# Four graph layers in one kernel: the opening's loads and order, the place of one division, and the engine of the last folds

## The chip, the cores and the metric

The kernel runs on one core of one Trainium2 chip. A core has five engines with an instruction queue each: TensorE (PE, its weight loads shown apart as PEld), VectorE (DVE), ScalarE (ACT), GpSimd (POOL) and SyncE (SP), which here only issues transfers. They run side by side and wait for one another through semaphores. The metric is the time on the device in microseconds (us), the median of several runs; lower is better.

## The reference

The input x is (8, 2048, 64): 8 graphs of 2048 nodes with 64 features, and one adjacency matrix `adj` (2048, 2048) of zeros and ones. Each of four layers normalises x over the features, applies a ReLU, computes a graph layer and adds its result to x.

```python
h = jnp.maximum(_layernorm(x, axis=-1), 0.0)
x = x + _L0_gnn_ref(h, H, adj, 64, W, W_ind, a_node, a_gn, a_ge, fcW, fcb, av)
...
h = jnp.maximum(_layernorm(x, axis=-1), 0.0)
x = x + _L3_gnn_ref(h, adj, embedding, weight, bias)
```

What matters of layer 0 and layer 3 here:

```python
# layer 0
industry = jnp.einsum('nm,bmf->bnf', adj / deg, x @ W_ind)
...
coefs1 = jax.nn.softmax(logits2, axis=-1)          # over the hyperedges e of node n
g = jnp.einsum('bne,benf->bnf', coefs1, all_he)
# layer 3
w = jnp.einsum('nd,dkio->nkio', embedding, weight)  # d = 16, k = 3
b = jnp.einsum('nd,do->no', embedding, bias)
As = [eye, A, 2.0 * (A @ A) - eye]
x_g = jnp.einsum('knm,bmc->bnkc', jnp.stack(As, 0), x)
out = jnp.einsum('bnki,nkio->bno', x_g, w) + b
```

Layer 1 is an attention over the neighbours, layer 2 three steps of a message passing with a small MLP.

## The kernel before

Nodes are cut into 16 tiles of 128 (NT = 16) and into 4 chunks of 512 columns (NCW = 4, CW = 512); the 8 graphs go in 4 pairs (NP = 4), since 2 x 64 features fill 128 partitions. The kernel is one long unrolled program. A scheduler places the instructions, except where order is kept by hand: through `InOrder` wrappers (V, A, G, S for VectorE, ScalarE, GpSimd, SyncE) and, for TensorE, through `kit.mm` and `kit.turn` while `kit.strict` is set. Transfers that SyncE and ScalarE issue go to their own queues[...].

**Opening** (lines 957 to 1071, in `layer0`). A loop over j normalises the x tiles (each 128 nodes x 8 graphs x 64 features), multiplies them by W_ind, splits the product into a rounded high part and a low rest, and multiplies both with the first 512 columns of the transposed adjacency matrix. One iteration j works on several tiles, each step with its own lag: `sums` and `centred` of tile j (VectorE, GpSimd), `squares`, `sums2`, `scales`, `scaled` of tile j-1 (ScalarE, VectorE), `turns` and `turned` of tile j-2 (four transposes on TensorE, copies on ScalarE), `maps` of tile j-3 (eight matmuls `py`), `halves` of tile j-4 (the split: a copy on ScalarE, then a subtraction on VectorE), and `spread` of tile j-5: eight matmuls into `acc`, each high part followed by its low rest, and one into `deg0` for the degrees. The tuple of steps is run in this order in every iteration, and each engine keeps to it. The row tiles `at` of the adjacency matrix come through GpSimd's queue, five of them in the pool; a new one is issued every second iteration.

The same loop makes the bias of layer 3, embedding times bias, as four chunks: `biases(c)` is 4 matmuls of a 16-row piece of the transposed embedding `eT[c]` with `bw` (each fp32 matmul is two instructions in the trace, as are the maps), and ScalarE copies the chunk from PSUM to `bs[c]`, right behind `squares`. The four `eT` come by four transfers (two on SyncE, two on ScalarE), into buffers of the list pool. The chunks use the four PSUM banks that `acc` takes over at j = 5.

**Pair lists** (`pairs_of` to `done`, loop from line 1441). 18 tiles of 114 nodes with 3 blocks of pairs each, 54 blocks. For each block: matmuls, `mixed` (two VectorE operations, one exponential on ScalarE), `weighed` (one VectorE operation and a product, on GpSimd for all but the last two blocks, which stay on VectorE), `gathered` (two instructions on TensorE, `pgs`, 5 blocks behind). After a tile's three gathers, `divided` multiplies by a reciprocal on VectorE (`gn`), `back` turns it (`ptg`), `done` copies to `hn`. The gather of a tile needs the PSUM buffer (one of two) that the division of the tile before last sets free. The division of tile 15 (LT - 3) stands at j = last + 2, behind the weighing of block 53.

**Kernel's end** (`layers23`, lines 2224 to 2287). For each graph pair p and node tile i, the weight products `u` are multiplied by the embedding on VectorE, added up to `fold` (lines 2269 to 2280), and three more additions on GpSimd (lines 2281 to 2283) end in `ot`, which SyncE stores. After all that, lines 2344 to 2348 sum up `kit.bad`, which tells whether the inputs are of the kind that the kernel is made for, and write `flag`. Each engine reads the flag (line 2349) and branches over a general version of the kernel, which is not run here. Line 2390 is the program's common end.

Of the kernel before, what the change touches and what calls it, by code (L numbers as in the profile page):

```python
# [8 lines left out]
FP = mybir.dt.float32  # L9
FR = mybir.dt.float32r  # L10
AF = mybir.ActivationFunctionType
# [5 lines left out]
P = 128  # L17
# [14 lines left out]
def cols(c, w=CW):  # L32
    return slice(c * w, (c + 1) * w)
# [742 lines left out]
def layer0(kit, hn, x1_dram, open_early, late_tile, between):  # L776
# [64 lines left out]
    with ExitStack() as sA:  # L841
# [115 lines left out]
        with ExitStack() as s1:  # L957
            sb = s1.enter_context(tc.tile_pool(name="nf_sb", bufs=2, reuse_waits="tile"))
            ps = s1.enter_context(tc.tile_pool(name="nf_ps", bufs=2, space=PSUM, reuse_waits="tile"))
            bw = lst.tile([P, B * F + 2 * B], FP, tag="hlo", name="bw", bufs=3)[0:16, 0:P]  # L960
            eT, pbs, bs = [], accs(), []
            for c in range(NCW):
                if c < 3:
                    eT.append(lst.tile([P, B * F + 2 * B], FP, tag="hhi", name="eT", bufs=3)[0:16, 0:CW])
                    bs.append(sb.tile([P, CW], FP, tag="bs", name="bs", bufs=3))
                else:
                    eT.append(lst.tile([P, B * F + 2 * B], FP, tag="hlo", name="eT", bufs=3)[0:16, 0:CW])
                    bs.append(lst.tile([P, B * F + 2 * B], FP, tag="hlo", name="bs", bufs=3)[:, 0:CW])

            def biases(c):  # L970
                for k in range(4):
                    kit.mm(pbs[c][:, k * P : (k + 1) * P], eT[c][:, k * P : (k + 1) * P], bw, start=True, stop=True)

# [59 lines left out]
            kit.use_ln_exp()  # L1033
            load(0)
            for h in range(2):
                A.dma_start(out=bw[:, half(h)], in_=t["L3_gnn_bias"])
            for c in range(NCW):
                (A if c > 1 else S).dma_start(out=eT[c], in_=t["embT"][:, cols(c)])
            for i in range(1, 4):
                load(i)  # L1040
            for g in range(2):
                at[g] = rows_of(0, g)
            kit.strict = True
            for j in range(NT + 5):
                on = lambda k: 0 <= j - k < NT
                for c in {1: (0, 1), 3: (2,), 4: (3,)}.get(j, ()):
                    biases(c)
                if j == 5:
                    acc = accs()
                if 9 <= j < 9 + NCW:  # L1050
                    S.dma_start(out=kit.bias_dram[:, cols(j - 9)], in_=bs[j - 9])
                if 1 <= j < 4:
                    at[j + 1] = rows_of(0, j + 1)
                if 0 < j and j + 3 < NT:
                    load(j + 3)
                if j == 6:
                    first = loads()
                for lag, step in (
                    (0, sums), (0, centred), (1, squares), (1, sums2), (3, maps), (4, halves),
                    (1, scales), (1, scaled), (2, turns), (2, turned), (5, spread),  # L1060
                ):
                    if on(lag):
                        step(j - lag)
                    if j in (1, 2, 4, 5) and step is squares:
                        c = j - 1 - j // 4
                        A.activation(bs[c], pbs[c], AF.Copy)
                m = j - 5
                if m > 0 and m % 2 and m // 2 + 5 < NT // 2:
                    at[m // 2 + 5] = rows_of(0, m // 2 + 5)
# [243 lines left out]
    with ExitStack() as s0:  # L1313
# [125 lines left out]
        for j in range(last + 2 * NB):  # L1439
# [13 lines left out]
            if 1 <= j <= last:  # L1453
                mixed(j - 1)
            if 3 <= j < last + 3:
                weighed(j - 3)
            if j == last + 2:
                divided(LT - 3)
                back(LT - 4)
# [547 lines left out]
def layers23(self, aT):  # L2007
# [181 lines left out]
    for p in range(NP):  # L2189
# [32 lines left out]


        y1 = sb.tile([P, N], FP, tag="y1", name="y1", bufs=1)
        yn, after = [None] * NCW, [None] * NCW
# [8 lines left out]
        for c in range(2, NCW):  # L2234
            acc = ps.tile([P, CW], FP, tag="acc", name="acc")
            spread(acc, y, c, True, every)
            nc.scalar.copy(y1[:, cols(c)], acc)
            weave.start(again(y1, c, yn))
        xn = None
        for c in range(NCW):  # L2240
# [13 lines left out]
            for k in range(4):  # L2254
# [24 lines left out]
                for h in range(2):  # L2279
                    nc.vector.tensor_add(fold[:, h], pr[h][:, 0:4, :], pr[h][:, 4:8, :])  # L2280
                nc.gpsimd.tensor_add(fold[:, :, 0:2, :], fold[:, :, 0:2, :], fold[:, :, 2:4, :])  # L2281
                nc.gpsimd.tensor_add(ot, fold[:, :, 0, :], fold[:, :, 1, :])  # L2282
                nc.gpsimd.tensor_add(ot, ot, xr[:, ks].rearrange("p (h f) -> p h f", h=2))
                nc.sync.dma_start(
# [11 lines left out]
def four_layers(  # L2296
# [13 lines left out]
    with ExitStack() as s:  # L2310
        keep = s.enter_context(tc.tile_pool(name="keep_f", bufs=1))
        dram = s.enter_context(tc.tile_pool(name="x_dram", bufs=1, space=DRAM))
        x1, x3 = (dram.tile([NP, P, N], FP, name=f"xd{k}") for k in (1, 3))
        kit = Kit(tc, t, keep)
        kit.bias_dram = dram.tile([P, N], FP, name="bias_dram")
        low = s.enter_context(tc.tile_pool(name="hn_f", bufs=1, reuse_waits="tile"))
# [26 lines left out]
        later[0].run(aT)  # L2343
        ps = s.enter_context(tc.tile_pool(name="flag_ps", bufs=1, space=PSUM))
        nc.vector.tensor_reduce(kit.bad[:, 0:1], kit.bad, AX.X, OP.add)
        pb = ps.tile([F, 1], FP, name="pbad")
        nc.tensor.matmul(pb, kit.ones, kit.bad[:, 0:1], start=True, stop=True)
        nc.vector.tensor_scalar(flag, pb[0:1, :], 0.5, None, op0=OP.is_lt)
    with tc.If(nc.values_load(flag[0:1, 0:1]) < 1):
# [44 lines left out]
```

## Time and profile before

| what | us |
|---|---|
| median of 3 runs | 1881.71 (1881.08 to 1883.15) |
| the profiled execution | 1880.27 |
| its span | 1878.1 |
| TensorE busy | 1840.7 |
| VectorE busy | 1174.5 |
| first spread of the opening begins | 23.55 |
| last division of the pair lists begins | 356.09 |
| last operation of VectorE ends | 1868.05 |

Busy time says how long an engine had an instruction in work. In a line of the order of time stand the start, the time, the engine, the source line (632 is that of the ordering wrapper, 737 that of `kit.mm`, 744 that of `kit.turn`), the operation, the tile written and the tiles read, the shape and the count, and in brackets how long the engine had been idle before it and what ended that. A line of the waits has who waited, for whom, us in total, times and the longest. "DMA" stands for a transfer. "POOLq" or "SPq" is the instruction sequencer of that engine: reads of the flag, branches, semaphores, the issue of transfers.

### The profile page before, as it was taken

The page shows a single profiled execution, that of the slowest core. Times are in us where ns is not written, and L with a number is a line of the kernel's source. Part 1 is how long each engine was busy: PE and PEld are TensorE (multiplying, and loading weights), DVE is VectorE, ACT ScalarE, POOL GpSimd, SP SyncE. Part 2 cuts the span into 40 slices and gives each one's busy share as a digit, 9 for nine tenths or more (in the row PEclk, how much of TensorE's full clock was granted, in tenths as well). Part 3 has the DMA queues.
Part 4 walks back from the last instruction along what each step waited for, and adds up shares of the span by engine and source line. Part 5 has one row for each costly group of instructions (what it writes and reads, how often), then busy time and mean ns, then how long its engine had stood idle before and what let it go on. Part 6 is the DMA issues. An engine that isn't in the chain of part 4 may idle for free.

```text
span 1878.1 us, 26150 instructions
## 1 busy us (share of the span) xinstructions
PE 1840.7 (98%) x10364; PEld 1146.9 (61%) x10364; DVE 1174.5 (63%) x1843; ACT 463.1 (25%) x1048; POOL 311.7 (17%) x435
## 2 busy tenths in 40 slices
PE   8999999899999999999999999999999999999997
PEld 7877767443333333577765577855677755777653
DVE  7766699789999999932446732357523275524465
ACT  5422455572222221121301112200112101113000
POOL 4211387220000000000111200012100021101122
PEclk9999999999999999999999999999999999999999
DMA  7666395383222222142101022101122011121000
GB/s 205 186 185 207 103 284 144 107 208 79 54 61 52 63 57 57 46 99 67 51 13 28 22 69 62 34 23 26 43 62 62 12 30 28 54 65 51 5 20 12
DMA packets 86372, 142.60 MB, mean 76 GB/s; under 512 B 33800, under 2 KB 34056, under 8 KB 83568
## 3 DMA queue, kind: packets, MB, share of 16 engines
q1 hardware_dynamic: 64976, 80.64, 14.8%
q0 software_dynamic: 21040, 56.98, 12.4%
q10 hardware_dynamic: 224, 3.22, 0.5%
q8 instruction: 83, 1.36, 0.3%
q14 instruction: 49, 0.40, 0.1%
HBM read 106.85 MB, written 37.09 MB: 77 GB/s over the span
## 4 chain that ended last, share of the span: by engine, by line
PE 50%; issue 10%; DMA 2%; POOL 2%; DVE 1%; POOLq 0%; ACT 0%; SPq 0%; DVEq 0%
PE acc L737 31%; PE u L737 14%; PE py L737 2%; PE pv L737 1%; POOL fold L2281 1%; PE var L737 1%; PE mean L737 1%; DMA xd<-e 0%; DMA W3f<-in_L_gnn_weight 0%; DMA den<-d_dram 0%; PE tx L744 0%; POOL ot L2282 0%; PE tv L744 0%; PE tp L744 0%; DVE pt L1807 0%
## 5 line engine op out<-in xcount | busy, mean ns | idle before, releaser
L737 PE MATMUL acc<-aT,parts 128*128 128x512 f32 x1664 | 441.3, 409 | 0.0
L737 PEld LDWEIGHTS acc<-aT,parts 128*128 128x128 f32 x1664 | 306.6, 188 | 97.7 <-issue 39.2
L737 PE MATMUL o<-pt,hS 128*32 128x512 f32 x2048 | 247.1, 593 | 2.0 <-DVE pt L632 1.2
L737 PE MATMUL u<-W3f,y 64*128 64x512 f32 x1024 | 241.3, 589 | 0.0
L2269 DVE TENSOR_TENSOR pr<-u,embf 128x512 f32<-128x512 f32 x256 | 170.6, 687 | 109.8 <-PE u L737 103.1
L1807 DVE SCALAR_TENSOR_TENSOR pt<-R,wd,aT 128x1024 f32<-128x1024 f32 x188 | 230.0, 1276 | 8.5 <-DMA R<-r_dram 5.2
L737 PEld LDWEIGHTS u<-W3f,y 64*128 64x128 f32 x1024 | 100.0, 187 | 119.8 <-issue 119.8
L737 PEld LDWEIGHTS o<-pt,hS 128*32 128x32 f32 x2048 | 79.1, 110 | 143.8 <-issue 112.8
L737 PE MATMUL dn<-pt,vd 128*32 128x512 f32 x1024 | 134.9, 593 | 0.0
L737 PE MATMUL u<-W3f,v 64*128 64x512 f32 x512 | 133.0, 596 | 0.0
L2281 POOL TENSOR_TENSOR fold<-fold 128x256 f32<-128x256 f32 x64 | 47.8, 746 | 495.8 <-DVE fold L2280 495.8
L2060 DVE TENSOR_TENSOR yb<-py,cb_f 128x512 f32<-128x512 f32 x32 | 22.1, 691 | 157.9 <-PE py L737 157.9
L1106 PE MATMUL acc<-at,Y 128*128 128x512 f32 x384 | 101.7, 405 | 0.3 <-ACT ev L1136 0.2
L737 PE MATMUL acc<-aTl,parts 128*128 128x512 f32 x384 | 99.7, 398 | 0.0
L2157 POOL TENSOR_TENSOR bq<-bq,xp 128x512 f32<-128x512 f32 x16 | 20.7, 1293 | 421.9 <-ACT xp L2140 421.9
L2273 DVE TENSOR_TENSOR pr<-pr 128x512 f32<-128x512 f32 x128 | 88.0, 688 | 2.2
L737 PEld LDWEIGHTS u<-W3f,v 64*128 64x128 f32 x512 | 56.5, 186 | 49.6 <-issue 36.3
L1807 DVE SCALAR_TENSOR_TENSOR pt<-R,wd,aTl 128x1024 f32<-128x1024 f32 x64 | 79.3, 1280 | 8.6 <-PE dn L737 3.9
L737 PEld LDWEIGHTS dn<-pt,vd 128*32 128x32 f32 x1024 | 40.7, 110 | 67.7 <-issue 49.2
L737 PEld LDWEIGHTS acc<-aTl,parts 128*128 128x128 f32 x384 | 71.5, 188 | 16.2
L1106 PEld LDWEIGHTS acc<-at,Y 128*128 128x128 f32 x384 | 68.5, 188 | 14.1 <-issue 0.8
L2074 DVE TENSOR_TENSOR parts<-tp,parts 128x512 fp32r<-128x512 f32 x16 | 11.1, 692 | 85.3 <-ACT parts L2073 85.3
(374 smaller groups left out, 2683.0 us busy)
## 6 DMA issues: line engine op xcount, KB each, us to landing
at<-in_adjT POOLq DMA_DIRECT2D x32, 512.0 KB, 4.6
raw<-in_adjT SPq DMA_DIRECT2D x64, 256.0 KB, 3.3
aT<-in_adjT POOLq DMA_DIRECT2D x12, 1024.0 KB, 7.5
xp<-xd SPq DMA_DIRECT2D x45, 256.0 KB, 2.9
R<-r_dram SPq DMA_DIRECT2D x14, 512.0 KB, 3.8
hhi<-hi_dram POOLq DMA_DIRECT2D x18, 235.1 KB, 4.3
hlo<-lo_dram POOLq DMA_DIRECT2D x18, 235.1 KB, 4.4
hi_dram<-hi SPq DMA_DIRECT2D x16, 264.0 KB, 3.1
```

The lines of the kernel that those rows point to most:

```text
L737: one = self.nc.tensor.matmul(*args, **kw)
L1106: mm(acc[p], Y[h][:, m, p, :], at[:, k, :], start=m + h == 0, stop=m == NT - 1 and h == 1)
L1807: V.scalar_tensor_tensor(pt, R, w, a.bitcast(FP), op0=OP.max, op1=OP.mult)
L2060: nc.vector.tensor_tensor(yb, py, bias[:, None, :].to_broadcast([P, 4, P]), op=OP.add)
L2074: nc.vector.tensor_tensor(lo, tp, hi.bitcast(FP), op=OP.subtract)
L2157: nc.gpsimd.tensor_add(bq, bq, xp)
L2269: nc.vector.tensor_tensor(a, u[h], emb[:, i, 8 * w : 8 * w + 8, None].to_broadcast([P, 8, F]), op=OP.mult)
L2273: nc.vector.tensor_add(pr[h], pr[h], a)
L2281: nc.gpsimd.tensor_add(fold[:, :, 0:2, :], fold[:, :, 0:2, :], fold[:, :, 2:4, :])
```

## The change

The opening: the embedding comes in one transfer of 16 rows into the memory of `M` (which is loaded only after the loop), at the head of ScalarE's queue; the four first x tiles lead SyncE's; the spread lags four tiles, not five, so that the loop has one iteration less; in iteration 1 the steps of the old tile come before `sums` and `centred` of the new one; the bias chunks are made in iterations 1 to 3 and copied in iterations 1 to 4. The pair lists' end: the division of tile 15 goes from j = last + 2, behind the weighing of block 53, to j = last, between `mixed` of block 53 and the weighing of block 51. The kernel's end: the last three additions are on VectorE for the last node tile of the last graph pair alone; the sum of `kit.bad` and the flag are made ahead of the last graph pair's last stage, in a PSUM buffer of that stage.

```diff
@@ -958,18 +958,16 @@
             sb = s1.enter_context(tc.tile_pool(name="nf_sb", bufs=2, reuse_waits="tile"))
             ps = s1.enter_context(tc.tile_pool(name="nf_ps", bufs=2, space=PSUM, reuse_waits="tile"))
             bw = lst.tile([P, B * F + 2 * B], FP, tag="hlo", name="bw", bufs=3)[0:16, 0:P]
-            eT, pbs, bs = [], accs(), []
+            eT, pbs, bs = M.rearrange("p t h e -> p (t h e)")[0:16], accs(), []
             for c in range(NCW):
                 if c < 3:
-                    eT.append(lst.tile([P, B * F + 2 * B], FP, tag="hhi", name="eT", bufs=3)[0:16, 0:CW])
                     bs.append(sb.tile([P, CW], FP, tag="bs", name="bs", bufs=3))
                 else:
-                    eT.append(lst.tile([P, B * F + 2 * B], FP, tag="hlo", name="eT", bufs=3)[0:16, 0:CW])
                     bs.append(lst.tile([P, B * F + 2 * B], FP, tag="hlo", name="bs", bufs=3)[:, 0:CW])
 
             def biases(c):
-                for k in range(4):
-                    kit.mm(pbs[c][:, k * P : (k + 1) * P], eT[c][:, k * P : (k + 1) * P], bw, start=True, stop=True)
+                for k in range(4 * c, 4 * c + 4):
+                    kit.mm(pbs[c][:, (k % 4) * P : (k % 4 + 1) * P], eT[:, k * P : (k + 1) * P], bw, start=True, stop=True)
 
             deg0 = ps.tile([P, CW], FP, tag="deg0", name="deg0", bufs=1)
             groups = lambda a: a.rearrange("p (g f) -> p g f", f=F)
@@ -1031,22 +1029,18 @@
                 kit.mm(deg0, ones_r, at[m // 2][:, m % 2, :], start=m == 0, stop=m == NT - 1)
 
             kit.use_ln_exp()
-            load(0)
+            A.dma_start(out=eT, in_=t["embT"])
             for h in range(2):
                 A.dma_start(out=bw[:, half(h)], in_=t["L3_gnn_bias"])
-            for c in range(NCW):
-                (A if c > 1 else S).dma_start(out=eT[c], in_=t["embT"][:, cols(c)])
-            for i in range(1, 4):
+            for i in range(4):
                 load(i)
             for g in range(2):
                 at[g] = rows_of(0, g)
             kit.strict = True
-            for j in range(NT + 5):
+            for j in range(NT + 4):
                 on = lambda k: 0 <= j - k < NT
-                for c in {1: (0, 1), 3: (2,), 4: (3,)}.get(j, ()):
+                for c in {1: (0, 1), 2: (2,), 3: (3,)}.get(j, ()):
                     biases(c)
-                if j == 5:
-                    acc = accs()
                 if 9 <= j < 9 + NCW:
                     S.dma_start(out=kit.bias_dram[:, cols(j - 9)], in_=bs[j - 9])
                 if 1 <= j < 4:
@@ -1055,16 +1049,18 @@
                     load(j + 3)
                 if j == 6:
                     first = loads()
-                for lag, step in (
-                    (0, sums), (0, centred), (1, squares), (1, sums2), (3, maps), (4, halves),
-                    (1, scales), (1, scaled), (2, turns), (2, turned), (5, spread),
-                ):
+                inputs, rest = [(0, sums), (0, centred)], [
+                    (1, squares), (1, sums2), (3, maps), (4, halves),
+                    (1, scales), (1, scaled), (2, turns), (2, turned), (4, spread),
+                ]
+                for lag, step in rest + inputs if j == 1 else inputs + rest:
+                    if j == 4 and step is spread:
+                        acc = accs()
                     if on(lag):
                         step(j - lag)
-                    if j in (1, 2, 4, 5) and step is squares:
-                        c = j - 1 - j // 4
-                        A.activation(bs[c], pbs[c], AF.Copy)
-                m = j - 5
+                    if 0 < j < 5 and step is squares:
+                        A.activation(bs[j - 1], pbs[j - 1], AF.Copy)
+                m = j - 4
                 if m > 0 and m % 2 and m // 2 + 5 < NT // 2:
                     at[m // 2 + 5] = rows_of(0, m // 2 + 5)
             kit.strict = False
@@ -1452,10 +1448,11 @@
                 next_nodes(i + 2)
             if 1 <= j <= last:
                 mixed(j - 1)
+            if j == last:
+                divided(LT - 3)
             if 3 <= j < last + 3:
                 weighed(j - 3)
             if j == last + 2:
-                divided(LT - 3)
                 back(LT - 4)
             if 5 <= j < last + 5:
                 gathered(j - 5)
@@ -2221,6 +2218,8 @@
             y = yn
 
 
+        if p + 1 == NP:
+            nc.vector.tensor_reduce(kit.bad[:, 0:1], kit.bad, AX.X, OP.add)
         y1 = sb.tile([P, N], FP, tag="y1", name="y1", bufs=1)
         yn, after = [None] * NCW, [None] * NCW
 
@@ -2236,6 +2235,10 @@
             spread(acc, y, c, True, every)
             nc.scalar.copy(y1[:, cols(c)], acc)
             weave.start(again(y1, c, yn))
+        if p + 1 == NP:
+            pb = ps.tile([P, CW], FP, tag="u0", name="pbad")
+            mm(pb[0:F, 0:1], kit.ones, kit.bad[:, 0:1], start=True, stop=True)
+            nc.vector.tensor_scalar(kit.flag, pb[0:1, 0:1], 0.5, None, op0=OP.is_lt)
         xn = None
         for c in range(NCW):
             xr = chunk_of(x3_dram[p], c)
@@ -2278,9 +2281,10 @@
                 ot = sb.tile([P, 2, F], FP, tag="ot", name="ot", bufs=1)
                 for h in range(2):
                     nc.vector.tensor_add(fold[:, h], pr[h][:, 0:4, :], pr[h][:, 4:8, :])
-                nc.gpsimd.tensor_add(fold[:, :, 0:2, :], fold[:, :, 0:2, :], fold[:, :, 2:4, :])
-                nc.gpsimd.tensor_add(ot, fold[:, :, 0, :], fold[:, :, 1, :])
-                nc.gpsimd.tensor_add(ot, ot, xr[:, ks].rearrange("p (h f) -> p h f", h=2))
+                own = nc.vector if p + 1 == NP and i + 1 == NT else nc.gpsimd
+                own.tensor_add(fold[:, :, 0:2, :], fold[:, :, 0:2, :], fold[:, :, 2:4, :])
+                own.tensor_add(ot, fold[:, :, 0, :], fold[:, :, 1, :])
+                own.tensor_add(ot, ot, xr[:, ks].rearrange("p (h f) -> p h f", h=2))
                 nc.sync.dma_start(
                     out=out[2 * p : 2 * p + 2, ns, :].rearrange("h p f -> p h f"), in_=ot
                 )
@@ -2312,6 +2316,7 @@
         dram = s.enter_context(tc.tile_pool(name="x_dram", bufs=1, space=DRAM))
         x1, x3 = (dram.tile([NP, P, N], FP, name=f"xd{k}") for k in (1, 3))
         kit = Kit(tc, t, keep)
+        kit.flag = flag
         kit.bias_dram = dram.tile([P, N], FP, name="bias_dram")
         low = s.enter_context(tc.tile_pool(name="hn_f", bufs=1, reuse_waits="tile"))
         hn = [low.tile([P, N], FP, tag=f"hn{p}", name=f"hn{p}") for p in range(NP)]
@@ -2341,11 +2346,6 @@
 
         ahead[0].run(aT, following)
         later[0].run(aT)
-        ps = s.enter_context(tc.tile_pool(name="flag_ps", bufs=1, space=PSUM))
-        nc.vector.tensor_reduce(kit.bad[:, 0:1], kit.bad, AX.X, OP.add)
-        pb = ps.tile([F, 1], FP, name="pbad")
-        nc.tensor.matmul(pb, kit.ones, kit.bad[:, 0:1], start=True, stop=True)
-        nc.vector.tensor_scalar(flag, pb[0:1, :], 0.5, None, op0=OP.is_lt)
     with tc.If(nc.values_load(flag[0:1, 0:1]) < 1):
         general(tc, t, out)
 
```

## The prediction

> **What bounds the kernel now.** I read the page first, for the share of each engine, then the waits and the order of time of the three stretches that the change touches. The page:
>
> ```profile
> PE 1840.7 (98%) x10364; PEld 1146.9 (61%) x10364; DVE 1174.5 (63%) x1843; ACT 463.1 (25%) x1048; POOL 311.7 (17%) x435
> ```
>
> TensorE is busy for all but 37 us of the 1878.1 us span. So only its few holes, its slow stretches and what follows its last matmul can be shortened; work saved on another engine counts only there. Busy times of the opening's steady part (us of the stretch; then PE, PEld, DVE, ACT, POOL; clock; DMA share; GB/s):
>
> ```profile
> 30.00:40.00 10.00, 10.00 (x63) 8.84 (x62) 9.65 (x15) 6.79 (x23) 4.49 (x6) 1.00 0.85 242
> ```
>
> PE has no hole there, and VectorE is nearly full too. The waits of the first 30 us, then the order of time:
>
> ```profile
> DVE st L632 <- DMA x<-in_xN: 6.1, 2, 5.2
> PE acc L737 <- DMA eT<-in_embT: 3.1, 1, 3.1
> ```
> ```profile
> 4.21 2.04 PE L737 MATMUL acc<-bw,eT 16*128 16x128 f32 x8 [4.21 <-DMA bw<-in_L_gnn_bias]
> 9.84 0.69 DVE L632 TENSOR_REDUCE st<-x 128x8 f32<-128x512 f32 x1 [5.19 <-DMA x<-in_xN]
> ...
> 10.78 0.68 DVE L632 TENSOR_REDUCE st<-x 128x8 f32<-128x512 f32 x1
> ...
> 20.24 1.16 PE L737 MATMUL py<-W_indf,hn 128*128 128x128 f32 x8
> ...
> 23.55 2.09 PE L737 MATMUL acc<-at,Y 128*128 128x512 f32 x8
> ...
> 26.95 2.08 PE L737 MATMUL acc<-at,Y 128*128 128x512 f32 x8
> ```
>
> The sum of x tile 1 (9.84) waits 5.19 us for its transfer, and the second sum of tile 0 (10.78), ready since the square ended at 6.44, stands behind it. The first spread starts at 23.55; the next 3.40 later, which is the steady pitch (26.95, 30.35, 33.76). The pair lists' end:
>
> ```profile
> 346.93 1.36 POOL L632 TENSOR_TENSOR mix<-ex,wt 128x512 f32<-128x512 f32 x1 [0.95 <-DVE ex L632]
> ...
> 350.08 1.28 DVE L632 TENSOR_TENSOR gn<-pgs,rden 114x512 f32<-114x512 f32 x2
> ...
> 350.91 2.02 PE L737 MATMUL pgs<-mix,S 128*114 128x512 f32 x2 [3.37 <-DVE gn L632]
> ...
> 356.09 0.69 DVE L632 TENSOR_TENSOR gn<-pgs,rden 114x512 f32<-114x512 f32 x1 [4.73 <-PE pgs L737]
> ```
> ```profile
> 351.00:354.00 3.00, 3.00 (x9) 1.84 (x10) 0.36 (x1) 0.27 (x2) 0.00 (x0) 0.50 0.02 5
> ```
>
> The gather of pair 51 waits 3.37 us for a division, and then runs at half the clock (0.50 in 351 to 354). Last, the instructions after the loop, by their line (duration, first and last start):
>
> ```profile
> L2349 POOLq TENSOR_LOAD <-flag x1: 497/497/497, 1869.4 to 1869.4; - x1
> L2349 SPq TENSOR_LOAD <-flag x1: 483/483/483, 1870.4 to 1870.4; - x1
> L2349 POOLq EVENT_SEMAPHORE  x1: 17/17/17, 1872.7 to 1872.7; - x1
> ```
> ```profile
> L2390 POOLq DRAIN  x3: 46/107/4482, 1872.8 to 1877.9; - x3
> ```
>
> GpSimd reads the flag only after its last folds, needs until 1872.7 to go on behind the branch, and then drains for 4.48 us; the span ends 0.84 after that drain.
>
> **What the Trainium skill says.** "TensorE: Matmul & The Clock Gate", section "What's actually happening": an idle TensorE runs at half rate until it has been busy for about one window of 3.4 us, and falls back after an idle one. The trace agrees: 2.04 us for eight small matmuls at 4.21, 1.16 at 20.24, and the 0.50 after the hole of 3.37. "SBUF — State Buffer", section "Who interferes with whom": a VectorE operation with two SBUF inputs and a GpSimd one that reads SBUF shut each other out. The trace agrees: the same normalisation takes 0.69 us at 34.02 and 2.00 at 36.78, beside GpSimd's centring. "GPSIMD Engine Reference", section 3.1: an fp32 add takes 1.96 times VectorE's time; here 0.73 against 0.41 us (128x256, lines 2281 and 2280), 1.8 times. "Runtime: NRT & Kernel Launch", section "Instruction fetch mechanics": a taken branch out of the fetched window waits for a fetch; here GpSimd's branch ends at 1870.05 and its next instruction starts 2.67 us later.
>
> **Opening.** Removed: four embT transfers and one loop iteration. Added: one transfer of 128 KB at the head of ScalarE's queue, ahead of the two bias rows. Moved: x tiles 0 to 3 to SP's head, past two embT issues (0.41 and 0.58 us); in iteration 1 the new tile's sums go behind the old tile's steps; biases 2 and 3 come an iteration earlier; the spread follows its split (`halves`) within one iteration. x tile 1 is issued near 1.2 instead of 3.75 and with some 190 GB/s (half of the 380 that all queues reach at 6 to 8 us) lands near 5; tiles 2 and 3 by 8, before they are wanted. Walking each engine's queue with the durations of the trace:
> - Tile 0 as before: sums 3.76, centred 4.74 to 5.78, square to 6.44. Bias rows land near 4.5 (issue 1.2 and 1.65, landing 2.4 to 2.9 later); 8 bias matmuls take 2.05, so the copy of chunk 0 is at 6.55 to 7.15 on ScalarE. Second sum 6.5 to 7.2, Ln and Exp to 7.8, scaled 7.85 to 8.55 (before 12.15).
> - Iteration 1's end and iteration 2: sums of tile 1 at 8.5, centred to 10.4, square and bias copy to 11.65, scales to 12.4, scaled to 13.15; PE does biases 2 and the turns of tile 0, ScalarE copies these to 13.2.
> - Iteration 3: square of tile 2, bias copy, scales to 15.2, scaled to 15.95; turned 1 to 16.0.
> - Iteration 4: square 3 and bias copy to 17.2, split of tile 0 on ScalarE to 17.8, on VectorE to 18.5. The first spread is at 17.8, at full pace from about 18.4.
> So 23.55 - 18.4 = 5.15 us earlier. But one more map and one more turn stand after that point: 0.89 + 0.36 us (pitch of their starts at 29.11, 30.00, 30.35). Net 3.9.
> Against it: the spread now waits on its own iteration's split. In steady state VectorE finishes one at 47.58, while PE reaches its spread at 47.42 and needs the second half at 47.66; every other iteration has 0.5 to spare. I take 0.05 us for 8 iterations, 0.4. Opening: 3.5. Ends: 5.2 if SP's head runs better, and -1 if the clock stays low until the spreads (two windows of 3.4 at half speed cost 3.4 to 5). Biases busy PE from 4.5 to 10.6 without a hole, so I expect the full clock before 13.
>
> **Pair lists.** One 0.61 us slot of VectorE moves ahead of pair 51's weighing. That weighing on GpSimd ends at 348.9 instead of 348.29; the division is done at 346.8. So the gather starts at 349.0, not 350.91, and PE's hole is 1.4 us, too short to lose the clock: gather to 350.0, turns of tile 15 to 350.5. The division of tile 16 still ends at 351.36, since VectorE has as much before it as ever; turns to 351.95, the last two gathers (1.88 at full clock) to 353.85, the last division at 353.9 against 356.09: 2.2 us. Ends: 1.0, if VectorE and GpSimd shut each other out for longer in the new order, and 2.4. ScalarE goes on at once (scores at 358.68 follow the last copy), so the shift stays.
>
> **End.** Three adds on VectorE after 1868.05: 0.41, and about 0.28 each for 128x128 (estimate from 0.69 for 512 and 0.41 for 256 elements), with 0.03 between: done at 1869.14 instead of 1869.92. The output is issued 0.8 earlier; SP's last drain comes at 1874.3 instead of 1875.09. GpSimd is now free at 1864.8 and reads a flag set long before: 0.5 + 0.05 + 2.67 bring it to its drain at 1868.1. If the drain takes 4.48 whenever it starts, it ends at 1872.6, SP is last, and the span ends at 1874.3 + 0.9: 3.0 saved. No row shows what the drain waits for; if it follows the others' end, 0.8 is left. I take 3.0, as the only work GpSimd had at hand is gone. The flag's matmul (0.28 us) moves from behind the last matmul onto PE's path: -0.3. Its reduction (0.23) and comparison (0.14) fall on VectorE while it waits for PE.
>
> Sum: 3.5 + 2.2 + 3.0 - 0.3 = 8.4. Against the profiled execution, 1880.27 (span 1878.1 and 2.2 around it), 1871.9; the runs' median is 1.44 higher, so 1873.3.
>
> **Rivals.**
> - The drain is tied to the others' end: 6.2 saved, 1875.5. For it: only the long drain is unexplained, the other two take 0.11 and 0.05. Chance 0.20.
> - The clock: by the walk above PE is busy for about half of 11 to 18 us; if the full clock is lost or never reached, the opening gives -1, and 1877.8 results. Against it: at 344 to 347 PE is 2.08 of 3.00 busy and keeps it. Chance 0.14.
> - Slower: the split decides. If GpSimd's centring shuts VectorE out ahead of every split instead of every second one after it, PE loses up to 1.3 us (2.00 - 0.69) in each of 16 spreads, 20.8: 1881.7 - 8.4 + 20.8 = 1894.1. It outweighs the rest from 0.53 us per spread on. For it: VectorE 9.65 of 10 busy. Against: GpSimd's centring stays queued behind its row transfer, which waits for PE to release a row tile every second iteration, so the place of the collision is tied to PE as before. Chance 0.07.
> - VectorE and GpSimd collide longer at the pair lists: 1874.5. Chance 0.06.
> The forecast itself: 0.53.
>
> **How the numbers follow.** 0.2% is 3.8 us, about what a measurement of this kernel can tell from no change: faster means below 1877.9. Forecast, tied drain, collision and half of the clock case: 0.86 faster; the other half 0.07 same; 0.07 slower. The range runs from all upper ends (5.2 + 2.4 + 3.2 - 0.2 = 10.6, so 1871.1) to the clock case (1877.8), with 1.0 on either side for the median, whose runs before span 2.1: 1870.1 to 1878.8. It leaves out the slow rival and little more.
>
> **What would show it.** First spread near 18, the pitch of 3.41 kept; the gather of pair 51 near 5 us before the last division instead of with a hole of 3.37, and no 0.50 clock; GpSimd's long drain starting before the last output is issued, and the span ending about 0.9 after SP's drain. Wrong: a pitch above 3.9, a first spread after 21, or a drain that again ends last.

## The result and the profile after

| | before | after |
|---|---|---|
| median, us (22 runs each) | 1882.24 | 1878.88 |
| lowest and highest | 1878.98 to 1885.37 | 1876.79 to 1881.78 |
| the profiled execution | 1880.27 | 1881.78 |
| its span | 1878.1 | 1879.7 |

The ratio of after to before is 0.9984, with a 95% interval of 0.9978 to 0.9990: the change saves 3.4 us in the medians, where 8.4 were forecast, and 1878.88 lies 0.1 above the upper end of the range. The profiled execution of after took as long as the slowest of its 22 runs, that of before less than the median of its own, so the two traces show where single steps moved, but not the difference of the medians. First the share of each engine, from the page of after (busy us, share of the span, instructions):

```profile
PE 1843.2 (98%) x10364; PEld 1146.9 (61%) x10364; DVE 1176.9 (63%) x1846; ACT 463.3 (25%) x1048; POOL 310.0 (16%) x432
```

TensorE has the same 10364 instructions and is busy for 2.5 us longer; three of GpSimd's instructions are now VectorE's. Next the start of the same TensorE work in both traces, after minus before. In order of time, the first matmuls of the stage behind the opening and the last `u` matmuls, of before, then of after:

```profile
73.75 1.08 PE L1106 MATMUL acc<-at,Y 128*128 128x512 f32 x4
...
1862.54 1.89 PE L737 MATMUL u<-W3f,y 64*128 64x512 f32 x8
```
```profile
76.76 1.08 PE L1102 MATMUL acc<-at,Y 128*128 128x512 f32 x4
...
1867.75 1.03 PE L737 MATMUL u<-W3f,y 64*128 64x512 f32 x4
```

The stage behind the opening starts at 76.76 instead of 73.75: 3.0 later, where 3.5 earlier was forecast. Ahead of the kernel's end, every stretch at half clock in these traces lasts 3.41 us or a multiple of it (6.82 in e3, 10.24 in after); this unit is called a window here, and a slow window is one at half clock. The gather of block 45 is 2.45 later, since before has a slow window from 217.54 to 220.96 and after has none there. From 382 on all is 4.0 later, up to the flag's matmul at 1754.68, which adds 0.38. From the last `u` matmul's end to the end of the span it takes 10.88 instead of 13.71. So the end came as forecast (2.83 for 3.0), and the opening and the pair lists did not.

The opening of after, in order of time:

```profile
0.73 0.88 SPq L632 DMA_DIRECT2D x<-in_xN  x2
0.77 0.41 ACTq L632 DMA_DIRECT2D M<-in_embT  x1
...
4.70 0.93 ACTq L632 DMA_DIRECT2D bw<-in_L_gnn_bias  x2
4.70 0.69 DVE L632 TENSOR_REDUCE st<-x 128x8 f32<-128x512 f32 x1 [1.90 <-DMA x<-in_xN]
...
9.82 5.45 PE L737 MATMUL acc<-bw,M 16*128 16x128 f32 x24 [9.82 <-DMA bw<-in_L_gnn_bias]
11.90 0.60 ACT L632 ACTIVATE bs<-acc 128x512 f32<-128x512 f32 x1 [4.52 <-PE acc L737]
...
13.04 0.69 DVE L632 SCALAR_TENSOR_TENSOR xc<-xc,st 128x512 f32<-128x512 f32 x1 [4.94 <-ACT st L632]
...
23.55 0.50 PE L737 MATMUL acc<-at,Y 128*128 128x512 f32 x1
...
24.27 1.88 PE L737 MATMUL acc<-at,Y 128*128 128x512 f32 x7 [0.22 <-DVE Y L632]
...
27.47 2.08 PE L737 MATMUL acc<-at,Y 128*128 128x512 f32 x8
```

ScalarE issues the embedding at 0.77 and then nothing until 4.70, though its queue has the two bias transfers next. 4.70 is when VectorE begins its sum of x tile 0, that is, when that tile has landed. The bias rows land at 9.40 and 9.73, and TensorE's first matmul is at 9.82 instead of 4.21. ScalarE copies the first bias chunk (11.90) ahead of the scales in its queue, so tile 0 is scaled at 13.04 (before: 12.15), and the first spread starts at 23.55, as before. From 27.47 on the pitch is 3.41, as before. The loop's tail in after, in order of time:

```profile
71.90 2.27 DVE L935 TENSOR_REDUCE bad<-MT 64x1 f32<-64x2048 f32 x1
...
73.58 0.40 PE L737 MATMUL acc<-at,Y 128*128 128x512 f32 x1
74.10 0.67 DVE L632 TENSOR_TENSOR Y<-py,Y 128x512 fp32r<-128x512 f32 x1
...
74.82 1.87 PE L737 MATMUL acc<-at,Y 128*128 128x512 f32 x7 [0.84 <-DVE Y L632]
```

The last spread waits 0.84 us for the low half of its split, which stands on VectorE behind a maximum over `MT`, a check of the inputs that the scheduler puts there. Before the change a whole iteration lay between them. The pair lists' end of after, in order of time, and the busy times of four clock windows around it (stretch, its length, then PE, PEld, DVE, ACT, POOL, clock, DMA share, GB/s):

```profile
348.57 0.68 DVE L632 TENSOR_TENSOR gn<-pgs,rden 114x512 f32<-114x512 f32 x1
...
350.00 1.36 POOL L632 TENSOR_TENSOR mix<-ex,wt 128x512 f32<-128x512 f32 x1 [1.55 <-DVE ex L632]
...
351.41 1.11 PE L737 MATMUL pgs<-mix,S 128*114 128x512 f32 x2 [1.40 <-POOL mix L632]
...
358.43 0.69 DVE L632 TENSOR_TENSOR gn<-pgs,rden 114x512 f32<-114x512 f32 x1 [4.59 <-PE pgs L737]
```
```profile
349.87:353.28 3.41, 1.65 (x8) 0.75 (x6) 3.34 (x5) 1.42 (x6) 1.36 (x1) 1.00 0.53 205
353.28:356.69 3.41, 2.71 (x7) 1.67 (x8) 0.55 (x1) 1.87 (x8) 0.00 (x0) 0.50 0.00 0
356.69:360.11 3.42, 2.54 (x6) 0.77 (x5) 0.69 (x1) 0.00 (x0) 0.00 (x0) 0.50 0.01 2
360.11:363.52 3.41, 3.41 (x9) 1.19 (x8) 0.69 (x1) 2.21 (x5) 0.94 (x1) 0.50 0.62 116
```

The division of tile 15 comes early (348.57), the gather of block 51 waits for GpSimd's weighing, and the hole is 1.40 instead of 3.37 us, all as forecast. Yet the clock still falls to a half, in this execution for three windows (353.28 to 363.52). From the gather of block 45 (338.45) to the last division (358.43) it takes 19.98 us; before, with one slow window, 20.10. The third slow window lies behind the last division and makes the shift to before still larger, from 2.3 us there to the 4.0 at 382. Last, the instructions behind the loop by line (count, shortest, median and longest ns, first and last start), and VectorE's last additions in order of time:

```profile
L2349 POOLq TENSOR_LOAD <-flag x1: 498/498/498, 1868.6 to 1868.6; - x1
L2349 SPq TENSOR_LOAD <-flag x1: 488/488/488, 1874.0 to 1874.0; - x1
L2390 POOLq DRAIN  x3: 46/107/4482, 1872.3 to 1879.4; - x3
L2390 SPq DRAIN  x3: 7/7/13, 1878.8 to 1879.1; - x3
```
```profile
1872.45 0.43 DVE L2285 TENSOR_TENSOR fold<-fold 128x256 f32<-128x256 f32 x1
1872.96 0.29 DVE L2286 TENSOR_TENSOR ot<-fold 128x128 f32<-128x128 f32 x1
1873.29 0.29 DVE L2287 TENSOR_TENSOR ot<-ot,xp 128x128 f32<-128x128 f32 x1
```

GpSimd reads the flag at 1868.6, before the last additions, and its long drain of 4.48 us runs from 1872.3 to 1876.8, ahead of SyncE's at 1878.8, which the end of the span now follows.

### The profile page after: what moved, and what is told of

Same layout as the page of the kernel before. It is cut to its first block, busy times and chain, and to the rows that moved or that the text cites. A ratio compares the mean times of both kernels' runs of the same rounds, so it can differ in the third digit from the quotient of the medians.

```text
span 1879.7 us, 26139 instructions
## 1 busy us (share of the span) xinstructions
PE 1843.2 (98%) x10364; PEld 1146.9 (61%) x10364; DVE 1176.9 (63%) x1846; ACT 463.3 (25%) x1048; POOL 310.0 (16%) x432
## 4 chain that ended last, share of the span: by engine, by line
PE 86%; issue 6%; DVE 4%; DMA 2%; ACT 1%; POOL 0%; SPq 0%; DVEq 0%; POOLq 0%
PE acc L737 34%; PE u L737 18%; PE o L737 8%; PE dn L737 4%; PE acc L1102 4%; PE py L737 3%; PE pd L737 2%; PE pgs L737 2%; PE mean L737 1%; PE pf L737 1%; PE var L737 1%; PE ph L737 1%; PE ph L1164 1%; PE pv L737 1%; DVE pt L1804 1%
```

## The experiments

Each time is a median, beside runs of the kernel before on the same chip; ratios are to the kernel before. A difference from after compares medians taken apart from each other: the kernel before had 1882.24 beside after, 1881.63 beside e1 to e4, 1881.33 beside e5 to e8 and 1881.37 beside e9 to e11, so up to 0.9 us of it can belong to the sessions.

**The bias rows first (e1).** Theory A: the bias transfers wait for an earlier transfer's end, and the opening is late for that. The orders of the instructions agree: in after, the two `bw` transfers are the ninth and tenth of SyncE's and ScalarE's together, and each carries a wait on one of eight completion semaphores, those of x tiles 0 and 1.

```text
after, ScalarE's queue
  DMACopy M<-in_embT 16x2048
  DMACopy bw<-in_L3_gnn_bias 16x64 [waits DMAHW0]
  DMACopy bw<-in_L3_gnn_bias 16x64 [waits DMAHW1]
with the bias rows first
  DMACopy bw<-in_L3_gnn_bias 16x64 x2
  DMACopy M<-in_embT 16x2048
```

The kernel before has the same wait in another place: there the ninth transfer is x tile 1, it waits for tile 0's semaphore, and it is issued just as VectorE can begin its sum of tile 0. Order of time, before:

```profile
3.75 8.06 SPq L632 DMA_DIRECT2D x<-in_xN  x5
3.76 0.69 DVE L632 TENSOR_REDUCE st<-x 128x8 f32<-128x512 f32 x1 [0.95 <-DMA x<-in_xN]
```

The prediction has this 3.75, but did not ask what the issue waited for.

```diff
-A.dma_start(out=eT, in_=t["embT"])
 for h in range(2):
     A.dma_start(out=bw[:, half(h)], in_=t["L3_gnn_bias"])
+A.dma_start(out=eT, in_=t["embT"])
```

> The changed kernel with the two transfers of the bias rows issued ahead of the embedding's on ScalarE's queue; nothing else. Theory A (the opening lost because the bias rows' transfers, ninth and tenth in order, had to wait for the landing of the first x tiles at 4.7 and 5.3 us and then landed at 9.4 and 9.7): the first bias matmul moves from 9.8 to about 4.6 us, the first spread from 23.5 to 18 to 20, and the kernel gains 4 to 6 us over the changed one (about 1873 to 1875). Rival B (the opening is held by the low clock of TensorE and by the spread's wait for its own iteration's split, not by the transfer): the first bias matmul moves, the first spread stays after 22, and less than 1.5 us is gained.

Measured: 1875.9 us, 0.9971 (0.9961 to 0.9980), 3.0 below after (2.4 by the ratios). In order of time, of this kernel:

```profile
0.77 0.88 ACTq L632 DMA_DIRECT2D bw<-in_L_gnn_bias  x2
1.67 0.44 ACTq L632 DMA_DIRECT2D M<-in_embT  x1
...
6.55 5.45 PE L737 MATMUL acc<-bw,M 16*128 16x128 f32 x24 [6.55 <-DMA M<-in_embT]
...
20.27 0.50 PE L737 MATMUL acc<-at,Y 128*128 128x512 f32 x1
```

Both bias transfers are issued at once and land at 3.17 and 3.91. The first bias matmul is 3.27 us earlier than in after, the first spread 3.28 and the next stage (73.50) 3.26: the delay goes through one for one. The 3.0 are less than A's 4 to 6, since the embedding, now behind, lands at 6.42 and is the late one. Rival B falls.

**Each part undone alone.** Three kernels: after with the opening of before, with the division of before, and with the end of before.

The opening's hunks undone (of them these lines and their companions):

```diff
-A.dma_start(out=eT, in_=t["embT"])
+load(0)
...
-for i in range(4):
+for c in range(NCW):
+    (A if c > 1 else S).dma_start(out=eT[c], in_=t["embT"][:, cols(c)])
+for i in range(1, 4):
     load(i)
...
-for j in range(NT + 4):
+for j in range(NT + 5):
```

> The opening as before; division and end as changed. Theory A (the changed opening costs 3.0 us): 3 us faster than the changed kernel, about 1876, 6 below the kernel before; at 220 us of the trace TensorE stands where it stood in the kernel before. Rival B (the changed opening is worth nothing either way, and the 3.0 us of the one profile are chance): within 1 us of the changed kernel.

```diff
-if j == last:
-    divided(LT - 3)
 if 3 <= j < last + 3:
     weighed(j - 3)
 if j == last + 2:
+    divided(LT - 3)
     back(LT - 4)
```

> The division of tile 15 back behind the weighing of block 53; opening and end as changed. Theory A (the earlier division saves 2.2 us, and a stretch at half clock took them back in the one profile): 2 us slower than the changed kernel in the median, about 1881, with the hole of 3.4 us ahead of the gather of block 51 back in the trace. Rival C (the earlier division makes TensorE's work sparser in a way that lowers the clock in nearly every run): as fast as the changed kernel within 0.7, or faster.

The end's hunks undone, the flag's and the additions':

```diff
-own = nc.vector if p + 1 == NP and i + 1 == NT else nc.gpsimd
+own = nc.gpsimd
...
-pb = ps.tile([P, CW], FP, tag="u0", name="pbad")
...
+ps = s.enter_context(tc.tile_pool(name="flag_ps", bufs=1, space=PSUM))
+pb = ps.tile([F, 1], FP, name="pbad")
```

> The kernel's end as before; opening and division as changed. Theory A (the drain of GpSimd takes 4.48 us whenever it starts, so taking it off the path saves what the two traces show, 8.2 against 11.0 us... that is about 2.7 us): 2.7 us slower than the changed kernel, about 1881.5, the drain last again. Rival D (only the three additions count): 0.8 us slower.

| kernel | median, us | ratio (interval) | above after |
|---|---|---|---|
| e2, old opening | 1876.58 | 0.9978 (0.9971 to 0.9985) | -2.3 |
| e3, old division | 1881.55 | 1.0000 (0.9991 to 1.0009) | +2.7 |
| e4, old end | 1880.52 | 0.9996 (0.9987 to 1.0005) | +1.6 |

So by the medians the new opening costs 2.3 us (A had 3, B less than 1), and the new division and the new end give 2.7 and 1.6. Added up that is 2.0 saved; 3.4 were measured, which the intervals of some 1.5 us on either side allow. Rival C falls with the 2.7.

That the opening costs time rests on the traces more than on the medians: the intervals of e2's ratio and of after's (0.9978 to 0.9990) overlap. With the new opening the next stage starts at 76.76, 76.85 and 77.01 (after, e3, e4), with the old one at 73.75 and 73.60 (before, e2). In e11, described below, whose opening is also the old one, it starts at 75.51: tile 0 is scaled as early as in before (12.01 for 12.15), but the full clock comes at 24.00 instead of 19.57. So the opening varies by up to 1.9 us, it seems with where the clock's windows fall, but does not reach 76.76.

In e4 GpSimd's drain ends last again, as in before, and from the last `u` matmul's end to the end of the span it takes 13.9 us (before 13.71, after 10.88). That speaks for A against D, though the median, 1.6, lies between their 2.7 and 0.8. In e3 the long hole is back, in order of time:

```profile
353.46 2.02 PE L737 MATMUL pgs<-mix,S 128*114 128x512 f32 x2 [3.37 <-DVE gn L632]
```

**All loads early (e5).** After, with both bias rows in one transfer on SyncE behind x tile 0, and the embedding still first on ScalarE; now the bias rows, the embedding and x tiles 0 to 3 are all among the first eight transfers, and none of them waits for another's end.

```diff
-for h in range(2):
-    A.dma_start(out=bw[:, half(h)], in_=t["L3_gnn_bias"])
-for i in range(4):
+load(0)
+S.dma_start(
+    out=bw.rearrange("p (h f) -> p h f", h=2),
+    in_=t["L3_gnn_bias"][:, None, :].to_broadcast([16, 2, F]),
+)
+for i in range(1, 4):
     load(i)
```

> The changed kernel with the bias rows in one transfer on SyncE's queue, second behind x tile 0 (the embedding stays first on ScalarE's). Theory A (both small loads must land early, nothing else holds the opening's start): both land near 4.5, the first bias matmul at 4.5 to 5, the first spread at 18.5 to 19.5, about 1 us faster than with the bias rows first (about 1875). Rival E (TensorE at half clock is the bound between the first bias matmul and the first spread: 32 bias instructions at 0.26, 16 of maps at 0.26 and 12 turns at 0.26 make 15.6 us): the first spread comes 15.5 us after the first bias matmul, at 20, and the time is within 0.7 of that kernel.

Measured: 1874.9 us, 0.9970 (0.9958 to 0.9982). In order of time:

```profile
4.78 5.48 PE L737 MATMUL acc<-bw,M 16*128 16x128 f32 x24 [4.78 <-DMA bw<-in_L_gnn_bias]
...
18.72 0.50 PE L737 MATMUL acc<-at,Y 128*128 128x512 f32 x1
...
67.12 2.27 DVE L935 TENSOR_REDUCE bad<-MT 64x1 f32<-64x2048 f32 x1
...
70.04 1.87 PE L737 MATMUL acc<-at,Y 128*128 128x512 f32 x7 [0.87 <-DVE Y L632]
```

The first spread is 4.8 us earlier than in after, 13.9 behind the first bias matmul (after: 13.7), and the next stage starts at 71.98. In all nine traces with the new opening and no work added to it this distance is 13.7 to 14.6, while the first bias matmul starts anywhere from 4.78 to 10.02. So in this opening the first bias matmul sets when the spreads start; theory E, with 15.5 and a first spread at 20, falls. The wait of 0.87 in the tail, behind the maximum, is still there.

**The check in its place (e6, e9).** The maximum over `MT` goes through the ordering wrapper, so that it stays behind the loop's work on VectorE (on top of e5); run once more on another chip.

```diff
-nc.vector.tensor_reduce(bad[0:E, 2:3], MT, AX.X, OP.max)
+V.tensor_reduce(bad[0:E, 2:3], MT, AX.X, OP.max)
```

> As the last one, and the maximum over MT on VectorE (line 935 of the changed kernel, 2.27 us, part of the input check) kept at its place in the program, after the opening, where the scheduler had put it ahead of the last tile's split. Theory A (with a lag of four the last spread waits 0.84 us for the split behind that maximum; in the kernel before an iteration lay between): no hole ahead of the last spread, 0.8 to 1.1 us faster than without. Rival (the maximum costs as much wherever it goes): no gain, within 0.3.

> The kernel with the bias rows on SyncE and the check moved, once more, beside the next two on one chip. Theory A: about 1872.5, between 1871.5 without and 1875 with a half-clock stretch at the end of the pair lists; at least a third of its runs at a mean clock of 0.997 or less.

Measured: 1871.89 us, 0.9950 (0.9937 to 0.9964), and on the other chip 1874.13 (about 1872.5 was expected), 0.9963 (0.9949 to 0.9976). The tail in order of time, in the first of the two:

```profile
67.64 0.69 DVE L632 TENSOR_TENSOR Y<-py,Y 128x512 fp32r<-128x512 f32 x1 [0.33 <-ACT Y L632]
...
68.89 1.99 PE L737 MATMUL acc<-at,Y 128*128 128x512 f32 x8
```

All eight matmuls run without a hole. From the first spread to the next stage it is 52.12 us instead of 53.26 in e5, so the tail was worth 1.1. The median is 3.0 below e5's, which the tail does not account for: 4 of e5's 6 runs have a mean clock of 0.996 or less, and 1 of e6's 5. On the second chip the profiled execution has no slow window at the pair lists; of its five timed runs one has a mean clock of 0.998, the others 0.995 or 0.996, so the slow clock is still met.

**Does the bias work count for the clock (e8)?** In after the 24 bias instructions keep TensorE busy from 9.82 to 15.27 without a break, and yet the full clock is first seen at 22.19. Counted back from there in steps of 3.41, the window from 11.95 to 15.36 holds hardly anything else. Here 12 matmuls of 128 rows (24 instructions; extra work into `deg0`, which is overwritten later) follow `biases(0)`, on top of e6. Theory G: matmuls of 16 rows don't count as work for the clock, full rows do. Rival H: they count alike.

```diff
 biases(c)
+for _ in range(12 if c == 0 else 0):
+    kit.mm(deg0[:, 0:P], kit.ident, kit.ident, start=True, stop=True)
```

> As the kernel with the check moved (turns not repeated), and 12 fp32 matmuls of 128 rows by 128 columns, of the identity with itself, into the buffer of the degrees behind the first chunk's bias matmuls: 12 x 0.52 = 6.2 us of work at half clock. Theory G (the 16-row bias matmuls do not count as activity for the clock, 128-row ones do): the full clock comes at 13.5 at the latest instead of near 19.5, and the first spread is no more than 2 us later than without, or earlier. Rival H (rows do not matter): the full clock stays near 19.5 or later, and the first spread moves back by 4 us or more.

Measured: 1874.39 us, 0.9965 (0.9954 to 0.9976). Order of time, then busy times:

```profile
7.07 5.49 PE L737 MATMUL deg<-ident_f 128*128 128x128 f32 x24
12.49 2.15 PE L737 MATMUL acc<-bw,M 16*128 16x128 f32 x16
...
15.16 1.18 PE L737 MATMUL acc<-bw,M 16*128 16x128 f32 x8
```
```profile
12.75:16.16 3.41, 3.41 (x28) 3.08 (x28) 1.44 (x3) 1.89 (x8) 0.00 (x0) 1.00 0.85 271
16.16:19.57 3.41, 3.04 (x15) 2.53 (x13) 2.36 (x6) 1.73 (x7) 1.04 (x1) 0.50 0.27 77
```

The full clock comes at 12.75, behind the full-row matmuls. In the next window TensorE is busy for all of its 3.41 us, mostly with 16-row matmuls (four turns, 0.66 us, stand among them), and the clock falls back for the window after it. G holds for the clock, H falls; whether the 16-row matmuls count for nothing or only for little, the runs do not tell. The detour costs more than it brings: the extra matmuls put the first spread 2.7 us later than in e6, where at most 2 were expected.

**The hole filled (e7, e10, e11).** What is the move of the division worth when the clock stays? On top of e6, the turns of list tile 14 are made three times and those of tile 15 twice, into the same buffers, to keep TensorE at work (also run on a second chip); and in the kernel before, the turns of tile 14 five times. The repeated turns are extra work.

```diff
-for p in range(NP):
-    kit.turn(d["pb"][:, p, 0:LN], gf[0:LN, p * P : (p + 1) * P])
+for _ in range({LT - 4: 3, LT - 3: 2}.get(i, 1)):
+    for p in range(NP):
+        kit.turn(d["pb"][:, p, 0:LN], gf[0:LN, p * P : (p + 1) * P])
```

> As the last one, and the turns of list tiles 14 and 15 issued three times and twice over into the same buffers, which fills TensorE's holes at the end of the pair lists with work that changes nothing. Theory A (the earlier division's gain is lost where a window of the clock finds TensorE idle too long): no half clock between 340 and 370 us, the last division 17.9 us after the gather of block 45 (17.86 in the one profile without half clock there, 20.0 in the two with), 1.5 to 3 us faster in the median. Rival F (the clock does not follow such holes, or the repeated turns only delay the gathers): half clock as before, and 0 to 1 us slower.

> The kernel with the turns repeated, once more. Theory A (the repeated turns keep the clock): no half clock between 340 and 370 us again, the last division 17.9 us after the gather of block 45, and a median 0.5 to 2 us below the last one's. Rival F (the one profile without half clock was chance): half clock there in this profile, medians alike.

In the kernel before, the same loop runs over `{LT - 4: 5}.get(i, 1)`:

```diff
-for p in range(NP):
-    kit.turn(d["pb"][:, p, 0:LN], gf[0:LN, p * P : (p + 1) * P])
+for _ in range({LT - 4: 5}.get(i, 1)):
+    for p in range(NP):
+        kit.turn(d["pb"][:, p, 0:LN], gf[0:LN, p * P : (p + 1) * P])
```

> The kernel before, with the turns of list tile 14 issued five times over, which fills the hole of 3.4 us ahead of the gather of block 51 with some 2.5 us of work that changes nothing. Theory A (the division's place costs 2.2 us at full clock, and what the half clock adds comes on top): no half clock between 340 and 370 us, the last division still 19 to 19.2 us after the gather of block 45 (20.10 in the kernel before, of which about 1 is the half clock), 0.5 to 1.5 us faster than the kernel before. Rival I (the hole cost its time only through the clock, and the earlier division would have won nothing by itself): 17.9 us.

Measured: 1871.82 us, 0.9956 (0.9942 to 0.9970), and 1872.32, 0.9951 (0.9938 to 0.9965), on the two chips; the kernel before, filled, 1879.29, 0.9991 (0.9983 to 0.9998), 2.1 below the kernel before where 0.5 to 1.5 were expected. No slow window is left at the pair lists in any of the three profiles. In the timed runs it is not always so: 2 of e7's 5 have a mean clock of 0.995, and 7 of e11's 17 one of 0.996 or less. The pair lists' end of before, filled, in order of time:

```profile
348.19 2.12 PE L744 MATMUL ptg<-ident_f,gn 114*128 114x114 f32 x20
...
352.12 1.08 PE L737 MATMUL pgs<-mix,S 128*114 128x512 f32 x2 [1.81 <-DVE gn L632]
...
355.74 0.69 DVE L632 TENSOR_TENSOR gn<-pgs,rden 114x512 f32<-114x512 f32 x1 [3.17 <-PE pgs L737]
```

From the gather of block 45 to the last division:

| kernel | division | half clock, us | us |
|---|---|---|---|
| before | old | 3.4 | 20.10 |
| e3 | old | 6.8 | 21.29 |
| before, filled (e11) | old | none | 18.54 |
| after | new | 10.2 | 19.98 |
| e1 | new | 10.2 | 19.97 |
| e2, e5, e6 | new | 3.4 | 19.25, 19.29, 19.52 |
| e4, e8, e9 | new | none | 17.87, 17.85, 17.85 |
| filled (e7, e10) | new | none | 17.86, 17.85 |

The filled kernel before, at 18.54, lies between the two theories, 19 to 19.2 and 17.9. At full clock the move is worth 18.54 - 17.85 = 0.7 us. It is no more because the division of tile 16, which the last two gathers stand behind, starts 14.69 us after the gather of block 45 in both orders (before, e11, e9), while the gather of block 51 moves from 14.92 to 12.95. The rest of the 2.2 forecast is the slow clock behind the hole, and the new order is spared that in part of the executions only. The mean clock of the runs shows the same: before never reached 0.998 in 86 runs for which it was recorded, after did in 9 of 22, e3, with the old division, in 1 of 14, and e11, with the old division and its hole filled, in 4 of 17. After's times go with it: 1877.5 at 0.998 (9 runs), 1878.4 at 0.997 (4), 1880.4 at 0.996 (6), 1881.5 at 0.995 (2); one run at 0.994 took 1880.5. The mean clock does not tell where a slow window lies: five profiles (before, e1, e4, e6, e8) have one between 216 and 225 as well.

Whether the repeated turns then help is not settled. On the first chip e7's median is 0.07 below e6's, where 1.5 to 3 were expected; on the second e10's is 1.8 below e9's, as expected. Without them the 10 runs on two chips have a median of 1872.93 (1871.3 to 1875.3), with them 1872.17 (1871.12 to 1874.58). The lowest ratios of all, 0.9950, 0.9951 and 0.9956, are those of e6 and of the two runs with the turns repeated: some 9 us below before.

## Why the prediction was right and wrong

Of the 8.4 us forecast 3.4 came. What is missing is the opening's: 3.5 were to be saved, and 2.3 to 3.0 were lost.

- *Opening, 3.5 saved: wrong, about 3 lost in the profiles, 2.3 in the medians.* The step that failed is "Bias rows land near 4.5 (issue 1.2 and 1.65, landing 2.4 to 2.9 later)". The landing times were read from before, where the bias rows led ScalarE's queue; I took a place in the queue for a time of issue. They were issued at 4.70 and 5.31, each upon the end of an x transfer, and landed 4.4 to 4.7 later, at 9.4 and 9.7. The orders of instructions show the wait; e1 and e5 confirm it, since without it the first bias matmul, the first spread and the next stage all move together. x tile 1, the reason for most of the expected gain, did come early (it landed at 5.29 instead of 9.82; tiles 2 and 3, forecast "by 8", at 9.48 and 10.06), and it did not matter: ScalarE's copy of the first bias chunk stands ahead of the scales.
- *"I expect the full clock before 13": wrong, by a second step.* "Biases busy PE from 4.5 to 10.6 without a hole" was right in kind, but such work, of matmuls of 16 rows, did not bring the full clock (e8). In e5, with everything else as the walk assumed, the first spread is at 18.7 for 17.8, with the full clock at 17.6.
- *The split's wait.* The first spread's second half waits about as predicted (18.4 after 17.8: 0.6; the trace has 0.5). The 0.4 us of stalls in the steady part did not come: the pitch is 3.41. What came is 1.1 at the tail, behind the maximum over `MT`, which the prediction did not look for (e6). After's 3.0 are thus: first spread 0, second half 0.5, one map and one turn more behind it 1.25, tail 1.1. With both removed (e6) the next stage starts at 70.95, 2.8 before the kernel before: the 3.5 was reachable but for 0.7.
- *Division, 2.2 saved: right in order, wrong on the clock, and the size is two things.* The hole became 1.4 as said, and GpSimd's weighing ended it. "PE's hole is 1.4 us, too short to lose the clock" is the step that failed here: in five of the eight profiles with the new order and no repeated turns the clock is lost at this place; in after the window 349.87 to 353.28 holds 1.65 us of work, and the clock falls behind it. Where the clock stays, the last division comes 17.85 us after the gather of block 45, for 17.9 forecast. But the 20.10 that this was set against holds 1.6 of half clock, so at full clock the move gives 0.7. Undone in e3 it costs 2.7 in the medians, near the forecast, since the old order loses the clock nearly always.
- *End, 3.0 saved and 0.3 lost: right.* 2.83 and 0.38. The drain has its 4.48 us wherever it starts, so the rival of a tied drain falls; the three additions took 1.17 for 1.09. In the medians e4 shows 1.6 for the two together, less than the 2.45 of the traces, with an interval of about 1.5 us on both sides.
- *The rivals.* The split did not decide (pitch 3.41). The clock rival, at 1877.8, came nearest in number, and a late full clock was part of it, but not the chief cause: in e5 the full clock still comes only at 17.63, and the opening gains. A rival that said the merged transfers wait for one another was missing.

## What to carry to other kernels

When transfers are merged, moved or put ahead of others, count how many are under way before the one that is needed first, and look whether it carries a wait for another's end: a place at the head of a queue is not a time of issue. Work that a scheduler places freely can land in the slack that a shortened lag took away, so look at both ends of a pipelined loop. A hole of nearly one clock window cost 1.6 us here through the clock, more than the 0.7 that closing a part of it won at full clock, and what shortens it brings the clock back only when the window that holds it keeps enough work.

## What the runs showed of the hardware

- A window of 3.41 us that TensorE filled, mostly with 16-row matmuls, lost the full clock (e8), and 5.45 us of them without a break did not bring it (after), while 128-row matmuls did (e8, 12.75). The Trainium skill, "TensorE: Matmul & The Clock Gate", section "What's actually happening", speaks of a busy or an idle window; here 16 rows against 128 made a difference too.
- At the pair lists' end, windows with 0.29 to 1.68 us of TensorE work lost the clock (before, after, e1, e2, e3, e5, e6), and windows with 1.76 (e8) or more kept it. At half clock, windows with 2.11 (e3), 2.54 and 2.71 us (after) did not regain it; 2.82 (e2) and 2.92 (e5) did. Busy time is not the whole rule: near 216, windows with 2.80 (e6) and 2.96 us (before) lost the clock, and one with 2.96 in e2 kept it. What decides there is open.
- A transfer of 16 rows of the bias took 2.4 to 2.7 us from issue to landing at a queue's head (e1), and 4.4 to 4.7 behind the embedding and x tiles (after).
- GpSimd's long drain took 4.48 us both where it starts 8.4 us after the last `u` matmul's end (before, 1872.8, behind its last additions) and where it starts 3.5 us after it (after, 1872.3, where these are gone).
